# Layer 1's pairs of exponential tiles added by accumulating DMAs in place of GpSimd

## The chip, the cores and the metric

The kernel runs on one core of one Trainium2 chip. The metric is the device time of one launch in microseconds (us). In what follows PE is TensorE, PEld its weight loads, DVE is VectorE, ACT is ScalarE, POOL is GpSimd and SP is SyncE, which here only issues DMAs.

## The reference

The reference is two layers of masked attention over 16 graphs of 1024 nodes with 256 features, in float32. Each layer normalizes, applies a ReLU, and adds the attention's output to its input. Layer 0 has 4 heads of 64 features, layer 1 has 8 heads of 32; layer 1 has biases on q, k and v as well.

```python
def _L1_gnn_ref(x, adjacency, Wq, bq, Wk, bk, Wv, bv, Wo, bo):
    ...
    q = heads(x @ Wq.T + bq)
    k = heads(x @ Wk.T + bk)
    v = heads(x @ Wv.T + bv)
    scores = jnp.einsum('bhnd,bhmd->bhnm', q, k) / math.sqrt(D)
    mask = adjacency[:, None, :, :] == 0
    scores = jnp.where(mask, -jnp.inf, scores)
    w = jax.nn.softmax(scores, axis=-1)
    out = jnp.einsum('bhnm,bhmd->bhnd', w, v)
    out = out.transpose(0, 2, 1, 3).reshape(b, n, e)
    return out @ Wo.T + bo
...
h = jnp.maximum(_layernorm(x, axis=-1), 0.0)
x = x + _L0_gnn_ref(h, adj, ...)
h = jnp.maximum(_layernorm(x, axis=-1), 0.0)
x = x + _L1_gnn_ref(h, adj, ...)
```

## The kernel before

The attention is computed transposed: keys lie on the partitions, 512 queries on the free axis. A group is one half of the queries (two of 512) and one half of the heads, so a batch has four groups in each layer. A group of layer 1 goes through eight steps, one for each tile of 128 keys, with its four heads side by side; a group of layer 0 goes through four steps, each with two tiles of keys for two heads. Every step makes one tile p of 128 x 2048 float32 (4 x 512).

A step has three parts. `scores` (L364) does four matmuls into two PSUM pairs. `exponentials` takes the minimum of the scores and the scaled mask on DVE (L380, in two halves) and the exponential on ACT (L385), in place in p. `weigh` (L396) multiplies p with v and accumulates in PSUM over the group. The tiles p come from two pools of buffers: even steps have three buffers, odd steps two (L376).

The denominators are the sums of p over the keys. They are made on PE by a matmul with a block of ones, `count` (L273). To halve that work in layer 1, each even tile and the odd tile that follows it are first added into one, and only the sum is counted (L471 and L472). Layer 0 adds its tiles in another way (`add_tiles`, L407 and L409, on DVE and POOL).

The order is written out by hand in `Stream.run`. The steps of all batches stand in one list: layer 0 of batch 0, then layer 0 of the next batch and layer 1 of this one in turn, to the last. Iteration i does the scores of step i, the weighting of step i-2 (LEAD is 2), the addition of the pair if step i-2 is an odd step of layer 1, and the exponentials of step i. What else there is to do is put on a list of due times by `later`: the count of a pair two iterations after its addition, and for each group the spread of its denominators through DRAM (L288 to L292), their reciprocals (L297 to L302), their check (L310, L311), the normalization on POOL (L316) and the output projection (L345). The input projections and the layer norms of the next batch and layer, the loads of adj (L121, POOL's queue, which converts them to bfloat16), their transposes by DMA (L125, SP's queue) and the conversion to a mask (L131) are put between the steps in the same way.

Each engine works through its own instructions in this order. An instruction waits on semaphores for what it reads and for the readers of what it overwrites. The addition at L471 overwrites the even tile, so it waits for the weighting of the even step and for the exponentials of the odd one. The count waits for the addition. The third odd step from a pair's own, counted from it as the first, takes the buffer of the pair's odd tile again, so its L380 waits for the addition too. The last group of the last batch (`hurry`) leaves out the addition of its last pair, so there are 16 x 16 - 1 = 255 additions.

Of the kernel before, what the change touches and what calls it, by code (L numbers as in the profile page):

```python
# [15 lines left out]
ALU = mybir.AluOpType  # L16
# [59 lines left out]
def fast_program(ctx, tc, a, w, loads, chk):  # L76
# [3 lines left out]
    nc = tc.nc  # L80
# [339 lines left out]
    class Stream:  # L420
# [38 lines left out]
        def count_steps(self, i, st):  # L459


            gr = st.gr
            if st.j % 2 == 0 and not (gr.hurry and st.j == NT - 2):
                return
            if gr.hurry and st.j >= NT - 2:
                if st.last:
                    self.counted(i, gr)
                gr.count(st.p, False, st.last)
            else:
                one = self.steps[i - LEAD - 1].p  # L470
                nc.gpsimd.tensor_add(one, one, st.p)  # L471
                self.later(i + 2, gr.count, one, st.j == 1, st.last)  # L472

        def counted(self, i, gr):
# [402 lines left out]
```

## Time and profile before

| What | Value |
|---|---|
| Time, median of 2 runs | 3462.5 us (3459.6 and 3465.4) |
| The profiled execution: its own time | 3465.9 us |
| The profiled execution: its span | 3464.0 us |
| Granted TensorE clock, mean | 0.997 |
| PE busy | 3402.7 us, 98% |
| DVE busy | 2465.9 us, 71% |
| ACT busy | 2177.0 us, 63% |
| POOL busy | 2447.1 us, 71% |
| Queue 1 (issued by SP) | 105.18 MB, 12.6% of 16 DMA engines |
| Queue 0 (issued by POOL) | 33.56 MB, 6.4% of 16 DMA engines |

The profile is of one execution. A group row names the line, the engine and the operation, what it writes and reads with the shapes, the count, and after the bar the busy time in us and the mean of one in ns; after the next bar stands the idle time of the engine just before these instructions, and what ended most of it. A queue row gives packets, megabytes and the share of the time of 16 DMA engines. A row of DMA issues gives the count, the size of one and the median us from issue to landing. In the timeline a row is the start in us from the begin of the span, the duration, the engine, the line and the operation, with a bracket that names the idle time before it and what ended it. The ends of matmuls are modelled, and PE can be shown as busy while it waits for a little.

### The profile page before, as it was taken

How to read it: one execution, taken by the hardware profiler on the slowest of the kernel's cores; microseconds unless marked ns; L12 is line 12 of the kernel's file. 1: busy time of each engine (PE TensorE's matmuls, PEld its weight loads, DVE VectorE, ACT ScalarE, POOL GpSimd, SP SyncE). 2: the span in 40 equal slices, each digit the busy share in tenths (PEclk: the TensorE clock that was granted, in tenths of full speed). 3: DMA queues.
4: the chain of work that ended last, by engine and by line, in shares of the span. 5: the costliest groups of instructions: out<-in, count | busy, mean ns of one | idle time of the engine just before them, and what ended most of it. 6: DMA issues, size and time to landing. Idle time of an engine off the chain costs nothing. (4 is left out here: it accounts for less than half of the span.)

```text
span 3464.0 us, 46246 instructions
## 1 busy us (share of the span) xinstructions
PE 3402.7 (98%) x18190; PEld 1283.5 (37%) x18190; DVE 2465.9 (71%) x2664; ACT 2177.0 (63%) x2402; POOL 2447.1 (71%) x1606
## 2 busy tenths in 40 slices
PE   7999999999999999999999999999999999999998
PEld 3333333333333333333333433333333333333332
DVE  4777767777677676777767777677776776767776
ACT  5556566675666756667566675666756666665665
POOL 4677676776677766777667776677767777776766
PEclk9999999999999999999999999999999999999999
DMA  6121221211112121121211221212121121120000
GB/s 134 40 42 33 47 38 35 50 37 45 35 35 50 41 41 35 38 48 40 46 37 36 44 41 44 38 36 44 40 47 35 47 41 35 47 38 20 11 17 30
DMA packets 250738, 141.77 MB, mean 41 GB/s; under 512 B 182416, under 2 KB 217488, under 8 KB 250512
## 3 DMA queue, kind: packets, MB, share of 16 engines
q1 hardware_dynamic: 232080, 105.18, 12.6%
q0 software_dynamic: 18432, 33.56, 6.4%
q8 instruction: 144, 2.36, 0.3%
q14 instruction: 82, 0.67, 0.1%
HBM read 120.33 MB, written 18.34 MB: 40 GB/s over the span
## 5 line engine op out<-in xcount | busy, mean ns | idle before, releaser
L380 DVE SCALAR_TENSOR_TENSOR p<-mask,ps 128x1024 f32<-128x1024 fp8e4 x1536 | 1797.3, 1214 | 687.3 <-PE ps L364 682.5
L385 ACT ACTIVATE p<-p 128x1024 f32<-128x1024 f32 x1536 | 1613.4, 1056 | 1000.0 <-DVE p L380 959.2
L471 POOL TENSOR_TENSOR p<-p,p 128x2048 f32<-128x2048 f32 x255 | 1160.6, 4553 | 349.4 <-PE po L396 274.6
L364 PE MATMUL ps<-qT,kT 32*128 32x512 f32 (+1 forms) x6144 | 1172.0, 633 | 15.2 <-ACT hT L196 6.8
L396 PE MATMUL po<-p,v 128*32 128x512 f32 (+1 forms) x6144 | 1043.5, 606 | 14.8 <-ACT o L280 14.2
L409 POOL TENSOR_TENSOR t<-t,t 128x1024 f32<-128x1024 f32 x192 | 468.7, 2441 | 447.5 <-DVE t L407 415.6
L364 PEld LDWEIGHTS ps<-qT,kT 32*128 32x128 f32 (+1 forms) x6144 | 378.1, 184 | 722.3 <-issue 359.5
L396 PEld LDWEIGHTS po<-p,v 128*32 128x32 f32 (+1 forms) x6144 | 205.0, 117 | 749.5 <-issue 466.7
L407 DVE TENSOR_TENSOR t<-p 128x1024 f32<-128x1024 f32 x192 | 286.2, 1491 | 4.5 <-POOL t L409 4.5
L273 PE MATMUL pz<-p,ones 128*32 128x512 f32 x2056 | 267.7, 593 | 0.0
L207 PE MATMUL pq<-hT,wk 128*128 128x512 f32 x512 | 240.9, 614 | 8.1 <-ACT hT L196 8.1
L236 PE MATMUL pv<-wv,hT 128*128 128x256 f32 x1024 | 237.9, 385 | 0.0
L207 PE MATMUL pq<-hT,wq 128*128 128x512 f32 x512 | 236.6, 605 | 0.0
L345 PE MATMUL py<-wo,cat 128*128 128x256 f32 x1008 | 234.6, 386 | 0.5 <-POOL cat L316 0.5
L236 PEld LDWEIGHTS pv<-wv,hT 128*128 128x128 f32 x1024 | 189.4, 190 | 75.2 <-issue 28.9
L345 PEld LDWEIGHTS py<-wo,cat 128*128 128x128 f32 x1008 | 186.3, 190 | 75.3 <-issue 27.5
L316 POOL TENSOR_TENSOR cat<-o,inv 128x512 f32<-128x512 f32 x127 | 164.7, 1297 | 23.2 <-DMA inv<-vd 17.1
L407 POOL TENSOR_TENSOR t<-p 128x1024 f32<-128x1024 f32 x64 | 151.7, 2370 | 2.8 <-ACT p L385 2.4
L207 PEld LDWEIGHTS pq<-hT,wk 128*128 128x128 f32 x512 | 93.7, 193 | 154.9 <-issue 117.8
L131 ACT ACTIVATE mask<-adjT,mhalf 128x1024 fp8e4<-128x1024 bf16 x128 | 145.6, 1139 | 2.3 <-DMA adjT<-adj 2.1
L207 PEld LDWEIGHTS pq<-hT,wq 128*128 128x128 f32 x512 | 92.2, 189 | 144.3 <-issue 130.5
L177 ACT ACTIVATE hn<-x,shift,rstd 128x256 f32<-128x256 f32 x256 | 138.1, 587 | 11.0 <-POOL shift L170 11.0
(52 smaller groups left out, 1615.5 us busy)
## 6 DMA issues: line engine op xcount, KB each, us to landing
adj<-in_adj_dram POOLq DMA_DIRECT2D x128, 256.0 KB, 3.7
x<-in_x_dram SPq DMA_DIRECT2D x32, 512.0 KB
inv<-vd SPq DMA_DIRECT2D x128, 128.0 KB
inv<-vd SPq DMA_DIRECT2D x252, 64.0 KB
out_dram<-x SPq DMA_DIRECT2D x31, 512.0 KB
adjT<-adj SPq DMA_TRANSPOSE x128
sd<-s SPq DMA_DIRECT2D x64, 4.0 KB
sn<-sd SPq DMA_DIRECT2D x64, 4.0 KB
```

What stands on the lines that cost most here:

```text
L207: nc.tensor.matmul(pq[:, m, :], wt[self.layer][:, c, ts(m, P)], self.hT[half][:, c, :], start=(c == 0), stop=(c == 1),)
L236: nc.tensor.matmul(pv[:, i, :], self.hT[half][:, c, ts(i, P)], w.v[self.layer][:, c, :], start=(c == 0), stop=(c == 1),)
L273: nc.tensor.matmul(self.s[r * self.D : (r + 1) * self.D, :], w.ones[:, : self.D], p[:, r, :], start=start, stop=stop,)
L316: nc.gpsimd.tensor_mul(self.half.cat[:, self.g, :], self.ob, self.inv)
L345: nc.tensor.matmul(py[:, i, :], self.half.cat[:, c, ts(i, P)], w.o[self.layer][:, c, :], start=(c == 0), stop=(c == 1),)
L364: nc.tensor.matmul(st.ps[i // 2][:, i % 2, :], gr.inp.kT[r * D : (r + 1) * D, gr.g, ts(kt, P)], gr.inp.qT[r * D : (r + 1) * D, gr.g, ts(gr ...
L380: nc.vector.scalar_tensor_tensor(out=half, in0=gr.mask.m[:, kt, ts(gr.qh, 512)].unsqueeze(1).to_broadcast([P, 2, 512]), scalar=BIG, in1=st ...
L385: nc.scalar.activation(half, half, AF.Exp, scale=gr.scale)
L396: nc.tensor.matmul(gr.o[r * D : (r + 1) * D, :], gr.inp.v[:, kt, h * D : (h + 1) * D], st.p[:, i, :], start=(kt == 0), stop=(kt == NT - 1),)
L407: engine.tensor_add(t, st.p[:, 0:2, :], st.p[:, 2:4, :])
L409: nc.gpsimd.tensor_add(t, t, gr.t)
L471: nc.gpsimd.tensor_add(one, one, st.p)
```

## The change

The addition of a pair in `count_steps` is no longer an instruction of POOL but a DMA from SBUF to SBUF that adds the odd tile to the even one at its destination. It is issued on POOL's DMA queue at the same place in the order. The pairs, the counts, the buffers and everything else stay.

```diff
@@ -468,7 +468,7 @@
                 gr.count(st.p, False, st.last)
             else:
                 one = self.steps[i - LEAD - 1].p
-                nc.gpsimd.tensor_add(one, one, st.p)
+                nc.gpsimd.dma_start(one, st.p, accum_op=ALU.add)
                 self.later(i + 2, gr.count, one, st.j == 1, st.last)
 
         def counted(self, i, gr):
```

Each of the 255 DMAs takes 128 x 2048 float32 (1 MiB) as its source and as many as its destination. The order of instructions on PE, DVE, ACT and POOL is the same as before, with the DMA issue in the place of the addition; the waits of L273 and L380 that were on POOL for the addition are now on the DMA's completion.

## The prediction

> **What bounds the kernel now.** I read the page from the top: busy time by engine, the groups, then the waits, then one stage of the timeline.
>
> ```profile
> span 3464.0 us, 46246 instructions
> PE 3402.7 (98%) x18190; PEld 1283.5 (37%) x18190; DVE 2465.9 (71%) x2664; ACT 2177.0 (63%) x2402; POOL 2447.1 (71%) x1606
> L471 POOL TENSOR_TENSOR p<-p,p 128x2048 f32<-128x2048 f32 x255 | 1160.6, 4553 | 349.4 <-PE po L396 274.6
> ```
>
> TensorE is busy for 3402.7 of 3464.0 us. POOL is busy for 2447.1, and 1160.6 of that are the 255 additions which the change moves. They come with 349.4 us of idle time before them, so POOL is not full. Whether anybody waits for them is seen in the trace's answer for line 471, under who waited:
>
> ```profile
>   PEld pz L273: 4.9, 16
>   DVE p L380: 3.4, 1
> ```
>
> 8.3 us in all. A POOL that never added these pairs would save 8.3 us, and TensorE leaves at most 61.3 us (3464.0 - 3402.7) to any change that takes no matmul away. What has to be asked is how late an addition may land. The timeline of the layer-1 stage of the fifth batch (start, us, engine, line) shows one pair:
>
> ```profile
> 1173.39 1.04 PE L396 MATMUL po<-p,v 128*32 128x512 f32 x5
> ...
> 1174.61 4.57 POOL L471 TENSOR_TENSOR p<-p,p 128x2048 f32<-128x2048 f32 x1 [2.26 <-PE po L396]
> ...
> 1175.81 1.06 PE L396 MATMUL po<-p,v 128*32 128x512 f32 x8
> ...
> 1180.14 2.40 PE L364 MATMUL ps<-qT,kT 32*128 32x512 f32 x8
> ...
> 1183.34 1.04 PE L273 MATMUL pz<-p,ones 128*32 128x512 f32 x8
> ...
> 1183.48 2.33 DVE L380 SCALAR_TENSOR_TENSOR p<-mask,ps 128x1024 f32<-128x1024 fp8e4 x2
> ```
>
> The addition can start when the weighting of the even step has read its tile (1173.39 + 1.04 = 1174.43). Two things fall due nearly together: the count of this pair on TensorE (1183.34), and DVE's write of the second odd step after this pair's own (1183.48), because odd tiles have two buffers and the addition still reads this one. The slack is 1183.48 - 1174.43 = 9.05 us; POOL uses 4.57 of it. The 254 pairs that have such a successor, read in the same way (ready is the later of the even weighting and the odd exponentials), give for the sixteen pairs of a batch 14.3, 13.4, 13.5, 13.5, 13.4, 10.8, 11.3, 13.5, 13.4, 11.0, 9.0, 11.9, 10.8, 9.3, 8.5 and 8.7 us. The batches with a following batch repeat this list, the last but one has two pairs at 6.7, and the last batch, which has little else on TensorE, has eight at 6.7 and five near 10. So: an addition that takes under about 8.5 us costs next to nothing, and one that takes more stops TensorE and DVE.
>
> **What the Trainium skill says.** "DMA: Bandwidth & Descriptors", section "SWDGE vs HWDGE vs iDMA": accumulation in a DMA must be issued by GpSimd, whose software writes the descriptors. The trace has 128 such software DMAs (the casting loads of adj), with 617 ns of POOL each. The same page, "Anatomy of one DMA", gives 2.0 us + bytes / 436 GB/s; for 1 MiB that is an estimate of 4.4 us for a copy. "Collectives: The Full Stack", section "The bandwidth ceiling: the fold count and why AG ≠ RS ≠ AR", says an adding DMA is slower than a copy because it reads two sources, at 31 GB/s per engine; from it I estimate 2 x 65,536 bytes / 31 GB/s = 4.2 us of transfer. No addition in a DMA is in the trace of before, so neither is confirmed. "SBUF — State Buffer", section "Who interferes with whom", says a DMA does not contend with compute engines; the casting loads show nothing against it.
>
> **The change, part by part.** Removed: 255 x 4553 ns = 1160.6 us of POOL. It was off the path, so the gain is the 8.3 us above at most; I take nothing.
>
> Added on POOL: 255 issues, by the nearest row 255 x 617 ns = 157 us. They are hidden in the time just freed. The wait for the even weighting and the exponentials stays the same, in the same place of POOL's order; behind it stand the normalization (L316), the checks of the sums and the next adj load, as before, and all get POOL earlier.
>
> Added to the 16 DMA engines: 255 DMAs of 1 MiB in SBUF, the latency being fixed part plus transfer. From these lines:
>
> ```profile
> q0 software_dynamic: 18432, 33.56, 6.4%
> adj<-in_adj_dram POOLq DMA_DIRECT2D x128, 256.0 KB, 3.7
> ```
>
> queue 0 wrote 33.56 MB of bfloat16 and so read 67.1 MB of integers, in 0.064 x 3464 x 16 = 3547 engine-us: 18.9 GB/s per engine. One load reads 32,768 bytes per engine, 1.7 us, of its 3.7 to landing: the fixed part is 2.0 us. An addition reads source and destination, 131,072 bytes per engine, and at 18.9 GB/s takes 6.9 us. The engines are not free in a layer-1 stage:
>
> ```profile
> 1089.00:1219.00 130.00, 128.90 (x794) 48.06 (x788) 87.63 (x93) 92.07 (x101) 98.63 (x58) 1.00 0.18 39
> ```
>
> The last columns are clock, DMA share and GB/s. With 0.18 to 0.19 of them taken, 6.9 / 0.81 = 8.6, and the latency is 2.0 + 8.6, about 10.5 us. That is over the slack of four pairs in a batch: 1.5 + 1.2 + 2.0 + 1.8 = 6.5 us. Fourteen batches make 91 us, the last but one 8, the last 33 (eight pairs lack 3.8 us each), in all 131 us. In the dense end of a stage pairs come every 7 us or so (1174.4, 1180.2, 1187.3, 1196.0, 1203.0, 1210.4), closer than 8.6, so the transfers queue; following the six through one queue gives 9 us per batch in place of 6.5, within the range.
>
> Both ends of the unknown: if the addition cost only one read, 3.5 us, the latency were 5.5 and nothing would wait. If the adder runs at half the read rate, 13.9 us, the DMA engines are the bound: sixteen pairs take 222 us in place of 130, and 16 x 92 = 1470 us come on top. I take the middle because the casting loads, which also convert on the way, were the only modified transfers to measure.
>
> Moved: nothing on any other engine; the order of PE, DVE and ACT is the same, only the waits at L273 and L380 are now on a DMA.
>
> **Sum.** The profiled execution took 3465.9 us; 3465.9 + 131 = 3597. The median of the two runs shown is 3462.5, 3.4 lower. I say 3595 us.
>
> **Rivals.**
> The transfer is hidden: latency up to 9.6 us. The same sum gives 62 us at 9.5 and 95 at 10, so at 9.6 it crosses 2% (69 us); below 8.5 it is under 20. For it: both estimates from the skill give 6 to 7 us (2.0 + 4.2, or 2.0 and 2 MiB / 436 GB/s = 4.8). Against it: the rate that queue 0 really had. It gives 3466 to 3530, and it is the case on the other side, for it ends not slower.
>
> The DMA engines become the bound: transfer with contention above 8.1 us, the mean distance of pairs in a stage (130 / 16), and clearly from 10 us on. At 10 us a stage takes 160 us and not 130; 16 x 30 = 480 us, 3945 in all. For it: nothing shows how fast DMA engines add in float32. Against it: queue 0 converted at the full read rate of its packets.
>
> The reciprocals come late: the chain of four small DMAs (sd, sn, vd, inv) shares the engines with the additions, and L316 already waits for inv 24 times (17.1 us). With an eighth of an addition (0.9 us) ahead of each, the chain is 3.5 us later; L316 holds up POOL, and the next addition is issued late. Where its slack is used up this is 2 to 3 us in each of 64 groups, 130 to 190 us, on top of 3595 as 3725 to 3785. I count it inside the first case's range.
>
> POOL gone from the path brings time: at most the 61.3 us without a matmul, 3403; over 2% would take more than all of it, unless modelled matmul ends hide waits.
>
> **How the numbers follow.** Latency case (9.6 to 12 us, its own range 3535 to 3785) 0.38; hidden 0.34; DMA-bound 0.25; gain 0.03. Faster by over 2% is 0.03, within 2% (about what a measurement of this kernel can tell from no change) 0.34, slower 0.63. The range from 3450 to 3950 holds the first two and somewhat under half of the third: 0.38 + 0.34 + 0.11 = 0.83.
>
> **What would show it.** Landing of L471's DMAs near 10.5 us and queue 0 far above 6.4%: right. Under 9: the hidden case, with waits of DVE L380 and PEld pz on it of a few us. Waits of L380 and L273 on the DMA should sum to 100 to 200 us and sit at the ends of the layer-1 stages and in the last batch; if they lie in every pair, the engines are the bound. POOL's busy time should fall by about 1000 us. If POOL stays as busy as before, the descriptors cost what the addition did, and my 617 ns is wrong.

## The result, and the profile after

The changed kernel takes 3670.8 us (median of 2 runs, 3663.5 and 3678.0) against 3462.5: 1.060 times the time before, with a 95% interval of 1.050 to 1.070. The forecast was 3595, in a range from 3450 to 3950, and slower was its likeliest side. The profiled span grew from 3464.0 to 3676.3 us, by 212.3; the forecast for it was 131. The page after, in the lines that answer to those of before:

```profile
span 3676.3 us, 46626 instructions
PE 3495.8 (95%) x18190; PEld 1294.3 (35%) x18190; DVE 2454.3 (67%) x2664; ACT 2171.6 (59%) x2402; POOL 1518.6 (41%) x1606
...
q0 software_dynamic: 55152, 300.97, 43.2%
q1 hardware_dynamic: 232080, 105.18, 12.0%
...
L471 POOL DMA_DIRECT2D p<-p x255 | 225.5, 887 | 535.0 <-ACT p L385 247.9
L316 POOL TENSOR_TENSOR cat<-o,inv 128x512 f32<-128x512 f32 x127 | 164.1, 1292 | 443.6 <-DMA inv<-vd 365.9
...
L310 POOL TENSOR_SCALAR ok_is_ge<-sn 128x8 f32<-128x8 f32 (+1 forms) x128 | 64.5, 504 | 305.9 <-DMA sn<-sd 299.4
...
p<-p POOLq DMA_DIRECT2D x255, 1024.0 KB, 7.9
```

Four things are to be seen. POOL lost 928.5 us of work, as intended. TensorE, with the same matmuls, is idle for 180.5 us where it was for 61.3 (119.2 more), and its busy time is 93.1 longer: together the 212.3. The addition lands 7.9 us after its issue, sooner than the 10.5 that I had forecast. And two waits of POOL, which nobody had moved, have become large: L310 (the check) for `sn` and L316 (the normalization) for `inv`, in the middle and at the end of a chain of small DMAs (`sd`, `sn`, `vd`, `inv`). The row for L316 before:

```profile
L316 POOL TENSOR_TENSOR cat<-o,inv 128x512 f32<-128x512 f32 x127 | 164.7, 1297 | 23.2 <-DMA inv<-vd 17.1
```

Its own work has not changed; what it waits for `inv` went from 17.1 to 365.9 us. Who waits for the additions themselves, from the trace's answer for line 471 after:

```profile
  DVE p L380: 57.7, 34
  PEld pz L273: 57.5, 39
...
DMA to landing us min/median/max: 6.9/7.9/12.8
```

These are the two places that the forecast names, and few waits, each of some microseconds. The rows must not be added up: the engines stand for the same landings at the same time. Laid over one another the waits cover 70.0 us, for 47 of the 255 additions; the others hold nobody up. The next view is the timeline after, in the layer-1 stage of the second batch, in a stretch that ends at 492.0 (start, us, engine, line):

```profile
469.11 0.87 POOL L471 DMA_DIRECT2D p<-p  x1
...
470.90 0.33 SPq L299 DMA_DIRECT2D vd<-vn  x1
...
477.28 1.12 SPq L302 DMA_DIRECT2D inv<-vd  x2
...
480.99 1.27 POOL L316 TENSOR_TENSOR cat<-o,inv 128x512 f32<-128x512 f32 x1 [8.83 <-DMA inv<-vd]
...
482.22 0.86 POOL L471 DMA_DIRECT2D p<-p  x1
...
490.25 1.07 PE L273 MATMUL pz<-p,ones 128*32 128x512 f32 x8 [1.61 <-DMA p<-p]
490.33 2.35 DVE L380 SCALAR_TENSOR_TENSOR p<-mask,ps 128x1024 f32<-128x1024 fp8e4 x2 [2.49 <-DMA p<-p]
```

Read it downwards. An addition is issued at 469.11. The reciprocals go out at 470.90 (`vd`), and can be fetched back (`inv`) only at 477.28, 6.4 us later. POOL stands at L316 for 8.83 us. The next pair was ready at 474.31, when its weighting ended, but POOL works in order and issues its addition only at 482.22, after L316 and 7.9 us late. It lands some 8 us after that, and then both TensorE (L273) and DVE (L380) have stood still for it. The same place in the kernel before:

```profile
463.09 0.33 SPq L299 DMA_DIRECT2D vd<-vn  x1
...
464.55 1.12 SPq L302 DMA_DIRECT2D inv<-vd  x2
...
468.25 1.26 POOL L316 TENSOR_TENSOR cat<-o,inv 128x512 f32<-128x512 f32 x1 [0.26 <-DMA inv<-vd]
```

Here `vd` to `inv` is 1.5 us, and POOL comes to L316 when `inv` is there but for 0.26 us. In the changed kernel 15 of the 127 steps from `vd` to `inv`, one in each batch but the last, had an addition under way before them; they took 5.3 to 8.2 us, most of them 6.4. The other 112 took 1.5 us as before (median).

The packet records of the trace say what the 6.4 us are. The 128 rows of 8192 bytes of the addition at 469.11 are eight for each DMA engine, one after the other, from 470.55 on, at first of 0.64 us each and at the end of up to 1.23; the last sixteen begin between 475.0 and 475.4 and end between 476.1 and 476.7. Of the 128 packets of `vd`, 32 bytes each and issued at 470.90 on another queue, two are recorded at 475.1 and 475.2, and 126 between 476.1 and 476.7: when the addition is through. The Trainium skill, "DMA: Bandwidth & Descriptors", section "Queues, rings and completion order", says that a DMA engine goes round the queues but drains a whole packet, of up to 64 descriptors, from one before it turns to the next. If the eight rows of an engine were one such packet, this would follow from it; the run with two halves, below, speaks against that reading, and why the rows go as they do stays open. What the trace shows is that a small DMA waits for the rest of an addition that is under way, not for a row of it.

POOL is not the only engine that waits for the chain. DVE takes the reciprocals of `sn` (L297) at their place between its other instructions, and stands there until `sn` has landed. From the view of waits after (us in total, times, longest):

```profile
DVE vn L297 <- DMA sn<-sd: 144.6, 49, 5.8
...
PE ps L364 <- DVE p L380: 79.9, 43, 4.4
```

Before, these two were 2.1 and 6.3 us. All 49 times an addition was under way when `sn` was issued. What it does is seen in the third batch's layer 1:

```profile
799.96 0.87 POOL L471 DMA_DIRECT2D p<-p  x1 [1.87 <-PE po L396]
...
804.11 0.35 SPq L292 DMA_DIRECT2D sn<-sd  x1
...
809.35 0.25 DVE L297 RECIPROCAL vn<-sn 128x16 f32<-128x16 f32 x1 [5.02 <-DMA sn<-sd]
...
810.74 3.20 PE L364 MATMUL ps<-qT,kT 32*128 32x512 f32 x8 [3.26 <-DVE p L380]
```

An addition is under way; `sn`, issued at 804.11, lands just before 809.35. DVE has stood for 5.02 us by then, its next L380 is late, and TensorE has a gap of 3.26 us that no addition ended. Sorted by what ended them, TensorE's gaps of over 0.3 us in this trace hold 78 us in which DVE had just stood for `sn` and TensorE went on with DVE's L380 (40 gaps), and 29 us that an addition's landing ended (26 gaps); before, there were none of either kind. So of the 119.2 us by which TensorE is longer idle, about two thirds come by way of DVE's wait for the small DMAs, and a quarter by late additions.

The last piece is TensorE's clock. The trace's table by stretches after, about the same gap (columns: us, busy time and count of PE, PEld, DVE, ACT and POOL, then the granted clock, the DMA engines' share and GB/s):

```profile
796.00:806.00 10.00, 9.50 (x80) 2.94 (x68) 6.64 (x6) 9.09 (x12) 5.33 (x3) 1.00 1.01 223
...
808.00:812.00 4.00, 1.26 (x6) 0.64 (x6) 2.46 (x3) 1.22 (x2) 1.92 (x5) 0.79 0.03 2
812.00:818.00 6.00, 6.00 (x26) 1.42 (x26) 2.35 (x2) 3.91 (x4) 0.00 (x0) 0.57 1.09 208
```

TensorE has its gap from 807.5 to 810.7, and as it ends the granted clock falls to a half, for 6.8 us. The record of the granted clock has 31 such stretches after, 157.8 us, and 3 before, 23.6 us; each is 3.4 or 6.8 us long (but for the last one of the launch), and after begins 1.7 to 5.2 us after the start of a gap of 1.2 to 4.4 us in TensorE's work. In 29 of the 31 that gap is one behind DVE's wait for `sn`; the other two lie at the end of the launch. At half clock half of the time is lost: (157.8 - 23.6) / 2 = 67 us. "TensorE: Matmul & The Clock Gate", part 1, says that the clock is set by activity in windows of 3413 ns that run freely: the lengths agree. It names an idle window of about 3.4 us as what brings the half clock; here gaps from 1.2 us on were followed by it. The length of a gap alone doesn't decide it: the 12 gaps of 1.2 to 2.8 us that an addition's landing ended were not followed by a half clock.

78, 29 and 67 us make 174 of the 212.3; I can't assign the rest.

### The profile page after: what moved, and what is told of

The parts are those of the page before. It is cut to its first block, busy times and chain, and to the rows that moved or that the text cites. A ratio compares the mean times of both kernels' runs of the same rounds, so it can differ in the third digit from the quotient of the medians.

```text
span 3676.3 us, 46626 instructions
## 1 busy us (share of the span) xinstructions
PE 3495.8 (95%) x18190; PEld 1294.3 (35%) x18190; DVE 2454.3 (67%) x2664; ACT 2171.6 (59%) x2402; POOL 1518.6 (41%) x1606
## 5 line engine op out<-in xcount | busy, mean ns | idle before, releaser
L380 DVE SCALAR_TENSOR_TENSOR p<-mask,ps 128x1024 f32<-128x1024 fp8e4 x1536 | 1794.4, 1212 | 743.8 <-PE ps L364 595.0
L364 PE MATMUL ps<-qT,kT 32*128 32x512 f32 (+1 forms) x6144 | 1215.3, 640 | 88.8 <-DVE p L380 79.9
L396 PE MATMUL po<-p,v 128*32 128x512 f32 (+1 forms) x6144 | 1065.0, 621 | 29.3 <-ACT o L280 29.1
L364 PEld LDWEIGHTS ps<-qT,kT 32*128 32x128 f32 (+1 forms) x6144 | 386.6, 186 | 840.2 <-issue 386.4
L471 POOL DMA_DIRECT2D p<-p x255 | 225.5, 887 | 535.0 <-ACT p L385 247.9
L316 POOL TENSOR_TENSOR cat<-o,inv 128x512 f32<-128x512 f32 x127 | 164.1, 1292 | 443.6 <-DMA inv<-vd 365.9
L273 PE MATMUL pz<-p,ones 128*32 128x512 f32 x2056 | 290.5, 639 | 29.3 <-DMA p<-p 29.3
L310 POOL TENSOR_SCALAR ok_is_ge<-sn 128x8 f32<-128x8 f32 (+1 forms) x128 | 64.5, 504 | 305.9 <-DMA sn<-sd 299.4
```

Of the source, the lines that this page charges most:

```text
L273: nc.tensor.matmul(self.s[r * self.D : (r + 1) * self.D, :], w.ones[:, : self.D], p[:, r, :], start=start, stop=stop,)
L316: nc.gpsimd.tensor_mul(self.half.cat[:, self.g, :], self.ob, self.inv)
L364: nc.tensor.matmul(st.ps[i // 2][:, i % 2, :], gr.inp.kT[r * D : (r + 1) * D, gr.g, ts(kt, P)], gr.inp.qT[r * D : (r + 1) * D, gr.g, ts(gr ...
L380: nc.vector.scalar_tensor_tensor(out=half, in0=gr.mask.m[:, kt, ts(gr.qh, 512)].unsqueeze(1).to_broadcast([P, 2, 512]), scalar=BIG, in1=st ...
L396: nc.tensor.matmul(gr.o[r * D : (r + 1) * D, :], gr.inp.v[:, kt, h * D : (h + 1) * D], st.p[:, i, :], start=(kt == 0), stop=(kt == NT - 1),)
L471: nc.gpsimd.dma_start(one, st.p, accum_op=ALU.add)
```

## The experiments

My theory for them, called the sum: an addition is late when its late issue plus its landing of 7.9 us exceed the slack of its pair. The issue is late because POOL waits for reciprocals whose DMAs stand behind whole additions. Taken over the 254 pairs, from the traces: the issue comes after the pair is ready by 318 us in all before and by 595 after (2.3 on the mean, over 2 us in 114 pairs, where it was 78). Delay plus 7.9 less the slack of before is positive in 77 pairs, 158 us in all. With 7.9 and no delay but the 0.57 us that every issue has, the sum would be 18 us. It is an estimate, with the slack of the trace before, and too large for what it describes: 47 additions were waited for, 70.0 us. It also leaves out DVE's wait for `sn`, which I hadn't seen when I planned the runs. The rivals: the long landing alone; the late reciprocals alone; the DMA engines' bandwidth. Each run below is compared with the kernel before, run beside it (3465.1 to 3465.9); differences are of medians.

**The reciprocals asked for later.** For three of the four layer-1 groups, and the last of layer 0, in batches 1 to 14, POOL's check and normalization are put two steps later in the order, both with the adding DMA and, as a control, with POOL's addition:

```diff
+            d = 2 if gr.layer != gr.last and 0 < gr.inp.b < B - 1 else 0
-            self.later(i + 3, gr.test)
+            self.later(i + 3 + d, gr.test)
...
-            self.later(i + (5 if gr.layer and not gr.last else 4), gr.normalize)
+            self.later(i + d + (5 if gr.layer and not gr.last else 4), gr.normalize)
...
-                self.later(i + (7 if gr.layer else 6), gr.end_half)
+                self.later(i + d + (7 if gr.layer else 6), gr.end_half)
```

> The changed kernel, with the check of the sums and the normalization of three of the four layer-1 groups and of the last layer-0 group of a batch put two iterations later (batches 1 to 14). Theory chain (the small DMAs for the reciprocals come late behind the additions, POOL waits for them in order, and so the next additions are issued late): POOL's waits for sn and inv, 299 and 366 us in the changed kernel, fall by more than half, and the time falls from 3671 to 3500 to 3580 us. Theory latency (7.9 us to landing is over the slack by itself): the issue of an addition comes no later than before anyway, so 3650 to 3680 us.

> The kernel before with the same later check and normalization as later_dma, as its measure. Nothing waits for the reciprocals in the kernel before but for 17 us of POOL: 3455 to 3480 us. If this order costs time by itself, it is the part of later_dma's 145 us that is not the DMA's: over 3490 us.

With the DMA it took 3610.5 us (1.045, 1.040 to 1.049), the control 3482.2 (1.005, 1.003 to 1.007). So the change costs 128 us in this order, where it costs 208 in its own: 80 us are gone with nothing done to the additions. The waits of POOL, from the view of waits (us in total, times, longest), against 365.9 and 299.4:

```profile
POOL cat L316 <- DMA inv<-vd: 214.1, 43, 9.8
...
POOL ok_is_ge L310 <- DMA sn<-sd: 49.5, 9, 9.3
...
DVE vn L297 <- DMA sn<-sd: 96.0, 48, 6.6
```

POOL's waits fell by 402 us in sum, and pairs that are late by the sum from 77 to 18, which leaves 41 us by it. The time missed the 3500 to 3580 that I expected: POOL's instructions were moved, but DVE's reciprocals were not. DVE still waits 96.0 us for `sn`, and TensorE is idle for 40 us after such waits (78 in the changed kernel) and for 19 us until additions land (29). The control has a price of 17 us of its own that I can't name. The direction is as the sum has it, the size is not.

**Narrower reciprocals.** The denominators lie on 16 partitions, and not on 128, while they are inverted, so each small DMA has an eighth of the rows:

```diff
-            self.n_f = self.per * 512 // P
+            self.n_f = self.per * 512 // 16
...
-            self.sn = small.tile([P, self.n_f], F32, tag="sn", name=f"sn_{self.n}")
+            self.sn = small.tile([16, self.n_f], F32, bufs=2, tag="sn", name=f"sn_{self.n}")
```

(`vn`, `ok` and `chk` in the same way; the three small tiles have one or two buffers here in place of four, in both kernels.)

> The changed kernel, with the denominators laid on 16 partitions in place of 128 for the check and the reciprocals, so that each of the DMAs sn and vd has 16 rows and not 128, one per DMA engine and not eight. Theory chain, with a small row waiting for one adding row of 0.64 us each time: the hops sn and vd lose up to 7 x 0.64 = 4.5 us each where an addition is under way, and the time falls to 3520 to 3600 us. If the small DMA waits for the whole addition ahead of it whatever its rows are: 3650 to 3680. Theory latency: 3650 to 3680 us.

> The kernel before with the denominators on 16 partitions, as the measure for narrow_dma. Reciprocals and checks take 0.5 us or so longer each: 3465 to 3490 us, so that narrow_dma is no better by its narrow rows than the changed kernel. If it is 3500 or more, the narrow rows cost time by themselves, and narrow_dma's difference to its measure is about as large as that of the changed kernel, 205 us.

3715.9 us (1.073, 1.071 to 1.075) with the DMA, 3490.8 (1.007, 1.006 to 1.009) without: the change costs 225 us here. That each row of a small DMA waits for one row of an addition, so that fewer rows would wait less, has fallen. In the timeline of the narrow kernel `vd` is issued at 480.00 and `inv` at 485.80: 5.8 us, with 16 rows in place of 128. All 15 steps from `vd` to `inv` that had an addition under way before them took 4.9 to 7.3 us; they wait for the rest of the addition.

**No chain in layer 1.** DVE takes the reciprocals of layer 1 straight from PSUM, on all 128 x 512 elements, and nothing goes through DRAM; the check of layer 1's sums is left out but for the last group. Here too both ways of adding:

```diff
+            if self.layer and not self.hurry:
+                self.inv = work.tile([P, 512], F32, tag="inv", bufs=1, name=f"inv_{self.n}")
+                nc.vector.reciprocal(self.inv, self.s)
+                return
```

> The changed kernel, with the reciprocals of layer 1 taken by DVE straight from PSUM (128x512, some 3.5 us each) and no small DMAs in layer 1; it leaves out the check of the sums of layer 1 but for the last group. Theory chain: the additions are issued on time but for the chain of the last group of layer 0, and the kernel is 20 to 70 us slower than the same kernel with POOL's additions (direct_pool). Theory latency: it stays 170 to 220 us slower than direct_pool.

> The kernel before, with the same direct reciprocals of layer 1, as the measure for direct_dma; it leaves out the check of the sums of layer 1 but for the last group. 63 reciprocals of 3.5 us are 220 us more on DVE, which has 40 us free in a layer-1 stage of 130 us and needs 14 more: 3460 to 3540 us under both theories.

3595.3 us (1.037, 1.035 to 1.039) with the DMA, 3545.8 (1.024, 1.023 to 1.026) without. DVE's longer reciprocals cost 80 us; on top of them the change costs 49.5 us and not 208. Without the chain the same additions

```profile
L322 POOL TENSOR_TENSOR cat<-o,inv 128x512 f32<-128x512 f32 x127 | 174.9, 1377 | 139.8 <-DMA inv<-vd 129.6
...
p<-p POOLq DMA_DIRECT2D x255, 1024.0 KB, 7.6
```

land about as late as before (7.6 against 7.9), and do a quarter of the harm. So the landing alone isn't the cause: most of the loss needs the small DMAs of layer 1. The run takes away both of the chain's ways at once, POOL's waits in layer 1 and DVE's for `sn` (144.6 us in the changed kernel, none here), and so it doesn't tell them apart. What is left fits the late additions: the waits for them cover 52.2 us (70.0), and TensorE is idle for 19 us until they land. Two reservations: layer 0 still has its chain (129.6 us of waiting for `inv`), and TensorE is idle for longer in the control already (88.0 us against 61.3), in which a part of the change's cost may be hidden.

**Shorter pieces.** Two adding DMAs of 128 x 1024, or four of 128 x 512, for each pair, so that a small DMA has less to wait for:

```diff
-                nc.gpsimd.dma_start(one, st.p, accum_op=ALU.add)
+                for k in range(4):
+                    nc.gpsimd.dma_start(one[:, k, :], st.p[:, k, :], accum_op=ALU.add)
```

> The changed kernel, with each addition issued as two DMAs of half the blocks (128x1024), one after the other on POOL's queue. Theory whole (a DMA engine serves all rows of one adding DMA before it turns to another queue, so that a small DMA of SP's queue waits for the whole of the addition ahead of it, some 5 us): the small DMA gets in between the halves and waits half as long; POOL's waits for sn and inv (299 and 366 us in the changed kernel) fall by about half and the time falls to 3560 to 3640 us, in spite of 0.9 us more on POOL for each pair. If queue 1 is not served until POOL's queue is empty: 3670 to 3700. Theory latency: two DMAs land no earlier than one, 3670 to 3700 us.

> As split2, with four DMAs of 128x512 for a pair. Theory whole: a small DMA waits some 1.4 us at most, the chain is nearly as fast as before; 3500 to 3600 us, unless the four issues of 0.9 us on POOL take that back. If queue 1 is not served until POOL's queue is empty, or the latency alone decides: 3670 to 3730 us.

3655.8 us (1.055, 1.053 to 1.057) and 3647.8 (1.053, 1.051 to 1.055): only 15 and 23 us better than the change, and outside the 3560 to 3640 and 3500 to 3600 that I expected. With four, the page and the waits have

```profile
L472 POOL DMA_DIRECT2D p<-p x1020 | 906.0, 1417 | 434.8 <-PE po L396 155.9
...
p<-p POOLq DMA_DIRECT2D x1020, 256.0 KB, 5.4
```
```profile
POOL cat L316 <- DMA inv<-vd: 190.3, 67, 7.5
...
DVE p L380 <- DMA p<-p: 141.2, 72, 8.3
```

POOL's wait for `inv` fell from 365.9 to 190.3, but I had not counted the issues: 906 us of POOL, 3.6 us for each pair in place of 0.9, and the pieces land 5.4 us after their own issue (median), the last of a pair 7.1. DVE now waits 141.2 us for the additions, up from 57.7. DVE's wait for `sn` is 107.3 us with two and 78.2 with four. Smaller pieces are got at the price of late landings; the runs do not tell against the sum, but not for it either.

They do show more of how the DMA engines take turns. With two halves issued before it, a step from `vd` to `inv` took no less time than with the whole (6.8 us against 6.4); with four quarters, 3.4. The packet records of the two halves show why, in 14 steps of 14: the 128 packets of `vd` begin 2.6 to 2.8 us after its issue, when the first half is through, and are then spread over the rows of the second half to its end, 6 us after the issue and more. So a small DMA gets in behind the large DMA that is under way, but from then on its rows and those of the next large one go side by side, and not eight rows of the one at a time.

**Half of the addition by DMA.** Two blocks of the four by DMA, two by POOL (`one[:, 0:2, :]` in the DMA, `tensor_add` on `one[:, 2:4, :]`); and then three by DMA and one by POOL:

```diff
-                nc.gpsimd.dma_start(one, st.p, accum_op=ALU.add)
+                nc.gpsimd.dma_start(one[:, 0:2, :], st.p[:, 0:2, :], accum_op=ALU.add)
+                nc.gpsimd.tensor_add(one[:, 2:4, :], one[:, 2:4, :], st.p[:, 2:4, :])
```

> Half of a pair (two of four blocks) is added by an accumulating DMA and the other half by POOL. The transfer is 2.7 us in place of 5.4 and the landing some 5.2 us, under every slack; POOL takes 0.9 + 2.3 us for a pair. Theory chain: a small DMA waits for half as much; 3480 to 3560 us. Theory latency: no wait is left, 3460 to 3480 us.

> Three of four blocks of a pair are added by DMA and one by POOL. Theory sum (what counts is the delay of the issue plus the time to landing, against the slack of 8.5 to 14 us; either alone fits): landing about 6.3 us; with the delays measured in the changed kernel some 28 to 45 of 254 pairs exceed their slack, by 24 to 56 us in all, and with the clock lost after gaps of TensorE the time is 3500 to 3555 us. If the loss went with the bytes that the DMA engines move, it would lie between half (3484) and the whole (3671): 3570 to 3590 us.

3484.4 us (1.005, 1.004 to 1.007) for the half and 3555.2 (1.026, 1.024 to 1.027) for three quarters: 19, 90 and 205 us for 2, 3 and 4 blocks. It isn't proportional: a line from 19 at two to 205 at four would give 112 at three. The landings are 4.7, 6.3 and 7.9 us. With each kernel's own delays the sum is 1 us for the half (2 pairs), 20 for three quarters (26 pairs) and 158 for the whole (77 pairs): too small by far at three quarters; 3555 lies at the very edge of the 3500 to 3555 that I gave for it. In this kernel the waits on the additions are small (13.9 us, laid over one another), and DVE's wait for `sn` is not:

```profile
DVE vn L297 <- DMA sn<-sd: 80.0, 31, 4.9
```

TensorE is idle for 32 us after DVE's waits for `sn` and for 8 us until additions land, and of the 90 us the half clock has 35: 17 stretches and 94 us of it, so (94 - 24) / 2.

**A plain copy in place of the addition.** The same DMA without its operation, which leaves out the addition of pairs but in the last group (and adds 1 to the denominators, so that none is zero):

```diff
-                nc.gpsimd.dma_start(one, st.p, accum_op=ALU.add)
+                nc.gpsimd.dma_start(one, st.p, **({'accum_op': ALU.add} if gr.hurry else {}))
```

> The changed kernel with plain copies in place of additions by DMA (it leaves out the addition of the pairs but in the last group, and adds 1 to every denominator in its copy out of PSUM on ACT so that they stay finite). It shows what the second read costs: if an adding row takes 0.64 us because it reads twice, a plain row of 8192 bytes takes 0.31 to 0.33 us, the landing is 5.2 us and queue 0 falls from 43% to 24% or so. Theory chain: the delays halve, 3500 to 3580 us. If the rows cost the same, 3660 to 3690 us.

3486.8 us (1.006, 1.005 to 1.008).

```profile
p<-p POOLq DMA_DIRECT2D x255, 1024.0 KB, 4.7
```
```profile
POOL cat L316 <- DMA inv<-vd: 279.3, 56, 8.0
...
DVE vn L297 <- DMA sn<-sd: 53.5, 33, 5.7
```

The same bytes are written. A row of 8192 bytes took 0.329 us and not 0.642 (median), and the DMA lands after 4.7 us. POOL still waits 484 us for the chain, three quarters of what it does with the addition, and this costs almost nothing: POOL's wait is no measure of the loss. DVE's wait for `sn` is down to 53.5 us, and TensorE is idle for 9 us after such waits. So the copy has a chain that is less late, and doesn't show what reciprocals as late as with the addition would cost with a short landing. With 4.7 in the sum, 1 pair is late.

**Half, with the reciprocals asked for later.** Both edits together, to see whether the 19 us of the half are POOL's waits.

> Half of a pair by DMA as in half, and the later check and normalization. Theory sum: half has hardly a pair over its slack (the rest of its 19 us is something else), so nothing changes: 3475 to 3490 us, less what later_pool differs from the kernel before. If the 19 us are POOL's waits for the reciprocals: 3462 to 3472 us.

3487.1 us (1.006, 1.005 to 1.008), the same as the half without. But its measure is the control in the same order (3482.2): the half costs 5 us here, where it costs 19 in its own order. In most batches the layer-1 stage takes 129.1 us against the control's 129.0; with the half in its own order it takes 128.2 to 129.9 against 127.5 in the kernel before. DVE's wait for `sn` is 8.2 us here and 44.3 in the half. So the 19 us may be waits for the reciprocals after all, but as the later order costs 17 us by itself, the run doesn't decide it. What the 21 us of the copy come from is open too; its layer-1 stages take about 1 us more each, like those of the half.

Nothing that was run beats the kernel before: TensorE is the bound there, and POOL, which all of them relieve, is not.

## Why the prediction was right, and where its steps were not

The side and the place were right: the additions were off the path, taking them from POOL gained nothing that can be seen, and in a late landing the count (L273) and the write of the odd tile (L380) have to wait. That the number came as near as it did, 131 us for 212, is in part luck: a landing put too long and a wait put at nothing made up for each other. The steps one by one:

- **POOL's work.** 1160.6 us removed, nothing gained: right. The issue was mis-sized: 887 ns and not 617, 226 us in place of 157, so POOL fell by 929 us and not by 1000. By itself it costs nothing that can be seen.
- **The slack** of a pair, from 14 down to 8.5 us and 6.7 at the end, was read rightly. That it sets a limit is seen in the 47 additions that were waited for.
- **The landing.** I put 10.5 us; it was 7.9. The transfer was the term at fault: 6.9, and 8.6 with the other traffic, where eight rows at 0.64 us make 5.1 us. The rate taken from the casting loads of adj, 18.9 GB/s, was too low; the addition reads 16,384 bytes in 0.642 us, 25.5 GB/s, and the copy 8192 in 0.329, 24.9. So the reason that "Collectives: The Full Stack" gives, section "The bandwidth ceiling: the fold count and why AG ≠ RS ≠ AR", two reads at one rate, holds here within 3% (0.642 / 0.329 is 1.95), though not its 31 GB/s. With 7.9 in my own sum, which has every issue on time, the answer would have been 12 us, which is "no change". The hidden rival had the landing right (below 9.6) and the time wrong.
- **The reciprocals.** I saw this chain, priced a hop at an eighth of an addition, 0.9 us, and the chain at 3.5. As a mean that was not too little: from the copy of the sums (L288) to the issue of the last `inv` it became later by 2.7 us in layer 1 (10.7 to 13.4) and by 1.1 in layer 0. But the delay isn't even: 112 of the 127 hops from `vd` to `inv` are as short as before, and one behind an addition waits for the rest of the whole, about 5 us more (6.4 against 1.5). And I named POOL's L316 as what waits. POOL's waits for `inv` and `sn` did go from 22 to 665 us, in part because POOL, relieved of the additions, comes to them earlier; the issues became later by 277 us in all.
- **DVE's wait for `sn`.** This is the step that failed. The prediction says that nothing moves on any other engine, and its chain ends at POOL; L297, the one instruction of DVE in the chain, stands in it at nothing. It waited 144.6 us, TensorE was idle for 78 us behind it, and 29 of the 31 stretches of half clock follow these gaps.
- **The sum.** I added 131 us for a long landing with punctual issues. The landing was shorter and the issues later, and what TensorE stood idle until an addition landed is 29 us. My separate range of 130 to 190 for the late reciprocals "on top of 3595" was near in size to what the chain costs (208 with it, 49.5 without that of layer 1), but not by way of the late additions alone, and on top of a landing that wasn't there.
- **The clock.** The sum had no term for it: 67 us more are lost at half clock after the gaps. No run changes the clock alone, so that the gaps bring the half clock is argued from their order in time, and not shown.
- **The DMA engines as the bound**: refuted. Queues 0 and 1 take 55% of them. The table by stretches has 0.78 over the layer-1 stage of the third batch, though 1.0 for 6 to 10 us at a time:

```profile
683.00:826.00 143.00, 131.90 (x782) 47.83 (x784) 85.36 (x91) 90.18 (x99) 40.83 (x58) 0.98 0.78 152
```

In this kernel the stage lasts 143 us where it lasted 127.5, and so the engines are free for some 31 of them.

- **The last batch.** Its layer 1 takes 142.5 us against 113.8: 29 us, where I had put 33. That is luck: I had eight additions late by 3.8 us each; four were waited for, some 9 us in all, and three gaps behind `sn` have 10 us more.

Shown by the runs: that the landing alone isn't the cause, and that most of the loss needs the chain of layer 1 (208 us with it, 49.5 without); that small DMAs wait for the rest of an addition under way. Read from the traces, and not shown by a run of its own: that the chain does its harm for the most part by DVE's wait for `sn` and not by late additions; no run moves L297 alone. Open: about 38 of the 212 us, the 20 us of the half and the copy, and the 17 us of the later order without DMAs.

## What to carry to other kernels

Before work is moved from an idle engine to DMAs, list every small DMA that some engine waits for in the same stretch, and allow for each the rest of a large DMA, not a share of it. Then list every engine that waits for it, and follow the wait through that engine's order to what TensorE needs next: here DVE's reciprocal stood before DVE's minima, and POOL's normalization before the next large DMA. Compare landing plus late issue with the slack of the buffer. The loss need not be proportional to the bytes: 2 of 4 blocks cost 19 us here, and all 4 cost 205. Where TensorE is the bound, look at the clock after its gaps too, as many of 1.2 to 4.4 us were followed by a half clock.

## What the runs showed of the hardware

- An adding DMA from SBUF to SBUF takes 0.642 us for a row of 8192 bytes, a copying one 0.329. 1 MiB lands after 7.9 and 4.7 us. For the copy, "DMA: Bandwidth & Descriptors", section "Anatomy of one DMA — SWDGE (gpsimd) path", would give 2.0 us + 1 MiB / 436 GB/s, 4.4 us by my estimate: near.
- POOL needs 887 ns to issue the adding DMA of 128 rows, 593 ns for the same as a copy, and 1417 ns for each of four in a row.
- A small DMA of another queue, with 16 rows or with 128, waited for the rest of a 1 MiB adding DMA that had begun: its hop took 5 to 8 us in place of 1.5. With the addition in two halves it got in behind the first, and its rows then went side by side with those of the second.
- The granted clock fell to a half for 3.4 or 6.8 us after 29 gaps of TensorE of 1.2 to 4.4 us behind DVE's waits, and after none of the 12 gaps of 1.2 to 2.8 us that ended with an addition's landing.
